# Row 0 of the outer points by four column products, with sums and doublings moved to accumulating DMAs

## The chip, the core and the metric

The kernel runs on one core of one Trainium2 chip. A core has a matmul engine (TensorE, PE), VectorE (DVE), ScalarE (ACT), GpSimd (POOL) and SyncE (SP), each with a queue of its own that it works off in order, and sixteen DMA engines. Accumulating DMAs are issued from POOL, plain loads and stores from SP. The metric is the time of one execution on the device in microseconds. The profile shows one further execution.

## The reference, cut to what matters

Two layers over x of shape (16, 128, 64, 64), each behind a group norm (32 groups):

```
x = x + conv(gn(x))        # 128 to 128 channels, 3x3; inputs quantized, v + 0.1 v^3; three weight sets
x = x + attention(gn(x))   # per position: exp(B) mixes exp(k) v and exp(k), times q, 128 x 64 products
# conv: mem = adc(o[2]) + 4 adc(o[0]) + 2 adc(o[1]) + adc(o[2]);  conv = mem * output_factor + bias
```

`o[i]` is the convolution of the same quantized input with weight set i. `adc` rounds and clips to an 8-bit-step value.

## The kernel before

**Tiling.** One image after another; channels lie on the 128 partitions. The 3x3 convolution is a fast convolution in rows: four output rows (r = 0 to 3) come from six *points* (0 to 5), each a combination of input rows. Points 1 to 4 are the inner ones, 0 and 5 the outer ones. Along a row, columns go in pairs, even and odd.

*Inner points* use four *column products* each. VectorE makes from a point the sums `cs`, the differences `cq` and the shifted differences `cd` of even and odd columns (L509 to L520), and PE forms four matmuls of 128x512 with weights `us` (q1, q2, q0, q3; `Block.half`, L569). *Outer points* use five matmuls: one on `sv`, the sum of even and odd columns (`pairs`, L522; `shared`, L620), whose result `spread` adds to both columns together with sums of the inner points (L623), and four on `v` (`outer`, L627).

For each image there are three *blocks*, one for each weight set. In the block's first part, PE makes points 2 and 1 (h = 0) and 4 and 3 (h = 1) in the PSUM tiles `pa` and `pb`; ACT copies partial sums (m1, sd, sA), and DVE combines them into `ss` (Bo, sm) and `ds` (df). The sum sm for h = 0 is an accumulating DMA on POOL (L596), that for h = 1 a DVE addition (L594). In the second part (`rest`, L645), rows 1 and 2 come from `middle` (ma, mc, L606), and rows 0 and 3 from the PSUM tile `py`:

| name | row 0 (k even) | row 3 (k odd) | engine |
|---|---|---|---|
| S0 / S3 | `total`: adds ss[0][:, 1] to ss[1][:, 1] | `total`: d0 + 8 d1 | DVE (L615, L618) |
| P | shared matmul | the same | PE |
| bc | spread: py + ss[1][:, 1] | py + d0 | DVE (L625) |
| o0, o1 | four matmuls | the same | PE |
| tk | take: py to int16 rows, every second element | the same | ACT (L633) |

The index k is 2i + h. The rest of block i of an image runs as k = 2, 3 (i = 0), 4, 5 (i = 1) and, in the turn of the next image, 0, 1 (i = 2). bA and bB clip the int16 rows (`bound`, L636). aA and aB (`add`, L640) double them on VectorE for block 0, which writes straight to `acc`, and add them to `acc` by an accumulating DMA for the others.

**Around it.** When `acc` is complete, ACT turns it into x (cx, L699), POOL adds the input by DMA (cd0x to cd3x, L702), ACT squares it (sq), DVE and PE make the norm (y0, ya to yd), and four pairs of tiles go through the attention (xn, kp, vp, ek, ekv, dn, g, u, ln, ex, oa, ob, oc, qp, op, r, rd, st; `Pair`, L734). `py` serves these pairs too (qp and op). At the same time the next image is loaded (li, lj), normalized (xa to xd), quantized (n), clipped (cl), made into values (s, va) and combined into rows (gr, er), points (pa, pb, p0, p5) and columns (cs, cq, cd, e0, e5).

**Order.** The order of all these operations is written out: `ORDER` (L38) is the steady turn of one image, `FIRST` and `LAST` the first and last images. A name with "+1" belongs to the turn before. Each engine gets its instructions in that order, so an instruction that waits holds all that stand behind it on its engine. In `Last` (L665) the last block of the last image uses `py` for row 0 and `pb` for row 3.

Of the kernel before, what the change touches and what calls it, by code (L numbers as in the profile page):

```python
# [38 lines left out]
    S3.2+1 cl1+1 q31.2+1 q10.3+1 cl0+1 P.2+1 sA1.2+1 q11.3+1 m10.3+1 bc.2+1 q20.3+1 o1.2+1 s1+1  # L39
    m11.3+1 s0+1 Bo.2+1 sd0.3+1 sq1+1 va1+1 lj3+1 q21.3+1 o0.2+1 va0+1 sd1.3+1 q30.3+1 sq2+1  # L40
    q00.3+1 q01.3+1 tk.2+1 lj2+1 sq3+1 df.2+1 er0+1 sA1.3+1 gr0+1 sA0.3+1 n3+1 P.3+1 ya+1 q31.3+1
    bc.3+1 pmy+1 yb+1 n2+1 q11.4+1 st2+1 sm.2+1 q10.4+1 pvy+1 m10.4+1 o1.3+1 o0.3+1 Bo.3+1 yc+1
    m11.4+1 df.3+1 yl+1 cp+1 yd+1 xn0+1 tk.3+1 ma.4+1 sm.3+1 q20.4+1 cl3+1 kp0+1 vp0+1 ek0+1
    q21.4+1 mc.4+1 st3+1 cl2+1 sd0.4+1 bA.2+1 s3+1 S0.4+1 P.4+1 li0 xn1+1 s2+1 sd1.4+1 ekv0+1
    bc.4+1 va3+1 q00.4+1 va2+1 dn0+1 g0+1 o0.4+1 o1.4+1 li1 q01.4+1 u0+1 ln0+1 oa0+1 tk.4+1 q30.4+1
    S3.4+1 kp1+1 gr1+1 qp0+1 vp1+1 ex0+1 sA0.4+1 sx0 sA1.4+1 ob0+1 q31.4+1 bA.4+1 sx1 oc0+1 ek1+1
    op0+1 er1+1 aA.2+1 q11.5+1 r0+1 q10.5+1 Bo.4+1 ekv1+1 m11.5+1 P.5+1 pa0+1 q21.5+1 x0 bc.5+1
    pb0+1 m10.5+1 dn1+1 q20.5+1 rd0+1 g1+1 sy1 o1.5+1 o0.5+1 st0+1 sd0.5+1 u1+1 oa1+1 cs0+1 df.4+1
    ln1+1 sd1.5+1 q00.5+1 ex1+1 tk.5+1 ob1+1 q30.5+1 cd0+1 qp1+1 q01.5+1 q31.5+1 sy0 xn2 oc1+1
    cq0+1 sA1.5+1 Bo.5+1 op1+1 kp2 sA0.5+1 bB.3+1 vp2 aA.4+1 q10.0 q11.0 df.5+1 r1+1 li3 bB.5+1 ek2  # L50
    m10.0 P.0 aB.3+1 sm.5+1 ekv2 sm.4+1 m11.0 q20.0 q21.0 rd1+1 dn2 mc.0 S0.0 sd0.0 sd1.0 q00.0
    bc.0 li2 g2 q30.0 sx3 aB.5+1 u2 oa2 pb1+1 o1.0 o0.0 ln2 pa1+1 sA0.0 ex2 sx2 q31.0 tk.0 q01.0
    ob2 st1+1 xn3 ma.0 qp2 kp3 oc2 op2 cs1+1 sy3 r2 vp3 S3.0 ek3 bA.0 sA1.0 q10.1 sy2 P.1 Bo.0
    q11.1 ekv3 m10.1 bc.1 dn3 cq1+1 aA.0 g3 o0.1 u3 o1.1 cd1+1 ln3 oa3 lj1 q20.1 ex3 m11.1 tk.1 ob3
    rd2 q21.1 qp3 lj0 bB.1 sd0.1 sd1.1 xa aB.1 q00.1 oc3 op3 q01.1 sA0.1 p0 r3 q10.2 sA1.1 e0 pmx
    df.0 p5 q30.1 rd3 q31.1 m10.2 cx0 e5 xb pvx sm.0 cx1 q11.2 y0 Bo.1 q20.2 cx2 xc m11.2 xl q21.2
    sd0.2 cd0x df.1 q00.2 cx3 sm.1 xd sd1.2 cd2x mc.2 q01.2 cd1x ma.2 S0.2 n1 cd3x sA0.2 n0 sq0
    q30.2
# [4 lines left out]
    hs0+2 x0+2 hq0+2 hs1+2 hq1+2 hq2+2 hq3+2 W0a+2 W0A+2 hs2+2 hs3+2 xa+2 W1a+2 pmx+2 xb+2  # L63
    pvx+2 W2a+2 xc+2 xl+2 hi+2 xd+2 W0b+2 W0c+2 hn1+2 hn0+2 W0e+2 W2A+2 hc0+2 hc1+2 W0d+2 W0f+2
    hn3+2 W2f+2 li0+1 hc3+2 hr1+2 hv1+2 hr0+2 hv0+2 li1+1 W2c+2 W0j+2 er0+2 hn2+2 W0g+2 W1A+2
    sx0+1 sx1+1 W0i+2 gr0+2 W0J+2 cp+2 W0k+2 hc2+2 hr3+2 W1c+2 W0h+2 W1b+2 x0+1 hr2+2 hv3+2
    W1e+2 W1J+2 hv2+2 W0n+2 W0l+2 hb+2 er1+2 sy1+1 W1f+2 gr1+2 W1j+2 li3+1 W0m+2 W0p+2 W0o+2
    pb1+2 hz1+2 hz0+2 sy0+1 li2+1 sx2+1 sy2+1 hcs1+2 hcs0+2 q11.0+1 hcq1+2 hcq0+2 pa1+2 sx3+1
    q10.0+1 sy3+1 m11.0+1 xa+1 W1d+2 W2b+2 hcd0+2 q21.0+1 cs1+2 m10.0+1 W1g+2 q20.0+1 sd0.0+1
    sd1.0+1 W2d+2 hcd1+2 lj0+1 W1h+2 q01.0+1 q30.0+1 q00.0+1 W2e+2 W2g+2 W1i+2 sA1.0+1 cd1+2  # L70
    sA0.0+1 pmx+1 W2h+2 q31.0+1 q11.1+1 m11.1+1 xb+1 cq1+2 q10.1+1 W1l+2 m10.1+1 q21.1+1 lj1+1
    Bo.0+1 W2J+2 pvx+1 W2j+2 q20.1+1 sd0.1+1 q00.1+1 sd1.1+1 q01.1+1 W1k+2 q30.1+1 df.0+1 xc+1
    W1m+2 q31.1+1 p0+1 xl+1 W1o+2 W1n+2 xd+1 sA0.1+1 e0+1 n1+1 P.2+1 sm.0+1 q10.2+1 W1p+2 W2i+2
    Bo.1+1 W2l+2 n0+1 sA1.1+1 df.1+1 q11.2+1 m10.2+1 q20.2+1 sd0.2+1 cl0+1 q00.2+1 sm.1+1
    m11.2+1 ma.2+1 q21.2+1 sA0.2+1 sd1.2+1 q10.3+1 mc.2+1 q01.2+1 p5+1 s0+1 cl1+1 S0.2+1
    q30.2+1 q31.2+1 va0+1 s1+1 S3.2+1 sA1.2+1 lj3+1 W2m+2 q11.3+1 W2n+2 m10.3+1 Bo.2+1 bc.2+1
    m11.3+1 q20.3+1 bA.2+1 va1+1 df.2+1 q21.3+1 lj2+1 e5+1 sd0.3+1 sd1.3+1 n3+1 o1.2+1 n2+1
    o0.2+1 q00.3+1 gr0+1 q30.3+1 q31.3+1 sA0.3+1 q01.3+1 tk.2+1 P.3+1 W2p+2 li0+0 er0+1 sA1.3+1
    W2o+2 q10.4+1 Bo.3+1 sm.2+1 cp+1 bc.3+1 df.3+1 q11.4+1 m11.4+1 o0.3+1 cl2+1 cl3+1 W2k+2
    sx0+0 sm.3+1 s2+1 va2+1 mc.4+1 ma.4+1 q21.4+1 m10.4+1 q20.4+1 sd0.4+1 o1.3+1 sd1.4+1 S0.4+1  # L80
    aA.2+1 x0+0 q30.4+1 li1+0 tk.3+1 S3.4+1 q00.4+1 sA0.4+1 q31.4+1 P.4+1 bc.4+1 s3+1 q01.4+1
    q10.5+1 Bo.4+1 o1.4+1 bB.3+1 va3+1 sx1+0 bA.4+1 er1+1 m10.5+1 q20.5+1 sA1.4+1 aA.4+1 sy1+0
    q11.5+1 m11.5+1 o0.4+1 gr1+1 sd0.5+1 li3+0 tk.4+1 sy0+0 q21.5+1 P.5+1 q00.5+1 sd1.5+1
    q01.5+1 df.4+1 pb0+1 sA1.5+1 q30.5+1 sA0.5+1 q31.5+1 bc.5+1 pa0+1 o1.5+1 Bo.5+1 cq0+1
    df.5+1 cs0+1 o0.5+1 li2+0 tk.5+1 P.0+0 q10.0+0 sm.4+1 m10.0+0 q11.0+0 m11.0+0 sm.5+1
    q20.0+0 sd0.0+0 q21.0+0 sd1.0+0 cd0+1 q01.0+0 mc.0+0 aB.3+1 S0.0+0 bB.5+1 bc.0+0 sx2+0
    pa1+1 ma.0+0 pb1+1 q00.0+0 sA0.0+0 q30.0+0 o0.0+0 S3.0+0 o1.0+0 sy2+0 q31.0+0 aB.5+1 cs1+1
    sx3+0 sy3+0 bA.0+0 aA.0+0 tk.0+0 P.1+0 sA1.0+0 q11.1+0 q10.1+0 m10.1+0 lj1+0 bc.1+0 o0.1+0
    Bo.0+0 m11.1+0 cq1+1 lj0+0 xa+0 o1.1+0 tk.1+0 cd1+1 bB.1+0 aB.1+0 q20.1+0 sd0.1+0 pmx+0
    xb+0 ho+2 q21.1+0 p5+0 sd1.1+0 q00.1+0 pvx+0 xc+0 q01.1+0 p0+0 sA0.1+0 df.0+0 q10.2+0  # L90
    sA1.1+0 q11.2+0 q30.1+0 xl+0 q31.1+0 m10.2+0 q20.2+0 m11.2+0 e5+0 e0+0 cx0+0 Bo.1+0 y0+0
    cx1+0 sm.0+0 cx2+0 sd0.2+0 df.1+0 cd0x+0 cx3+0 q21.2+0 cd1x+0 cd2x+0 q00.2+0 xd+0 sd1.2+0
    sm.1+0 mc.2+0 q01.2+0 sA0.2+0 n1+0 n0+0 q30.2+0 ma.2+0 sq0+0 cd3x+0 S0.2+0
# [4 lines left out]
    cl0+2 sA1.2+2 S3.2+2 q31.2+2 lj3+2 st2+2 q10.3+2 cl1+2 P.2+2 bc.2+2 m10.3+2 q11.3+2 m11.3+2  # L98
    s0+2 q20.3+2 q21.3+2 o0.2+2 Bo.2+2 va0+2 s1+2 va1+2 sd0.3+2 o1.2+2 bA.2+2 sd1.3+2 q01.3+2
    sq1+2 sq2+2 lj2+2 gr0+2 sq3+2 q30.3+2 q00.3+2 tk.2+2 sA1.3+2 er0+2 q31.3+2 sA0.3+2 ya+2  # L100
    df.2+2 n3+2 n2+2 pmy+2 yb+2 P.3+2 bc.3+2 Bo.3+2 cp+2 q11.4+2 pvy+2 q10.4+2 yc+2 cl3+2
    df.3+2 o0.3+2 m10.4+2 m11.4+2 o1.3+2 q20.4+2 q21.4+2 yl+2 s3+2 yd+2 xn0+2 sd0.4+2 sd1.4+2
    kp0+2 vp0+2 sm.3+2 tk.3+2 P.4+2 q01.4+2 cl2+2 sm.2+2 ek0+2 va3+2 mc.4+2 s2+2 st3+2 aA.2+2
    S0.4+2 ekv0+2 bc.4+2 dn0+2 sA1.4+2 g0+2 q00.4+2 sA0.4+2 va2+2 u0+2 xn1+2 ln0+2 o1.4+2 gr1+2
    o0.4+2 q30.4+2 oa0+2 ex0+2 kp1+2 er1+2 tk.4+2 qp0+2 ob0+2 vp1+2 q11.5+2 ma.4+2 oc0+2 S3.4+2
    ek1+2 m11.5+2 pb0+2 op0+2 r0+2 ekv1+2 q31.4+2 Bo.4+2 rd0+2 q10.5+2 pa0+2 m10.5+2 st0+2
    P.5+2 q20.5+2 df.4+2 bc.5+2 sd0.5+2 q21.5+2 sd1.5+2 dn1+2 q00.5+2 g1+2 bB.3+2 xn2+1 bA.4+2
    q01.5+2 q30.5+2 o1.5+2 o0.5+2 u1+2 cs0+2 oa1+2 ln1+2 cd0+2 q31.5+2 ex1+2 tk.5+2 sA1.5+2
    sA0.5+2 cq0+2 aB.3+2 sm.4+2 kp2+1 qp1+2 vp2+1 ob1+2 ek2+1 aA.4+2 Bo.5+2 oc1+2 q10.0+1 op1+2
# [34 lines left out]
def conv_preact_kernel(  # L144
# [29 lines left out]
    P = 128  # L174
# [21 lines left out]

    v = buf("v", 2, T, RW)
    cd = buf("cd", 4, T, 2 * W2)  # L200
    cs = buf("cs", 4, T * W2)
    cq = buf("cq", 4, T * W2)
# [755 lines left out]
```

## Time and profile before

| | us |
|---|---|
| runs | 1602.0, 1598.37, 1602.01 (median 1602.0) |
| the profiled execution, its own time | 1598.49 |
| its span, first to last instruction | 1596.8 |
| PE busy in the span | 1487.7 |
| VectorE busy | 1479.8 |
| ScalarE busy | 1183.0 |
| GpSimd busy | 224.0 |

The granted TensorE clock is 0.981 over the span, and 1.00 in the stretch from 349.1 to 1305.4 us. DMA moved 227 MB, 42.1% of the sixteen engines' span on the queue that POOL writes (software) and 17.9% on SP's (hardware).

How to read it: busy time is the union of an engine's instructions; neighbours overlap a little, so the step from one start to the next is shorter than a duration. One float32 matmul of the program is two records on PE. Waits are put down to what ended last. A DMA's landing time runs from its issue to its end.

### The profile page before, as it was taken

The numbers are of one execution on the slowest core, as the hardware profiler recorded it, in microseconds if no ns is written. First come the engines' busy times: TensorE is split into PE (matmuls) and PEld (weight loads), VectorE is DVE, ScalarE is ACT, GpSimd is POOL, SyncE is SP. The second block draws the span as 40 slices with busy tenths as digits, with TensorE's granted clock in tenths as the row PEclk, the third lists the DMA queues.
The fourth block names the chain that finished last, engine by engine and source line by source line (L and its number), as shares of the span: only waits on it lengthen the run. The fifth ranks groups of instructions, "written<-read, shape, count | busy, mean of one in ns | idle before, by whom it ended". The sixth has DMA issues, their size and how long they took to land.

```text
span 1596.8 us, 14936 instructions
## 1 busy us (share of the span) xinstructions
PE 1487.7 (93%) x4680; PEld 563.4 (35%) x4680; DVE 1479.8 (93%) x1919; ACT 1183.0 (74%) x1857; POOL 224.0 (14%) x250
## 2 busy tenths in 40 slices
PE   1798999999999999999999999999999999999985
PEld 0233433333333333333333343333333333333321
DVE  7999999999999999999999999999999999998775
ACT  7656878787777878778787877878778787766655
POOL 2001011121201112020111201111120111202010
PEclk6899999999999999999999999999999999999998
DMA  6235467594746758465684746659474675836462
GB/s 186 79 92 120 103 160 171 126 204 114 148 128 164 184 119 196 120 137 141 150 205 109 156 131 150 166 132 203 117 152 132 156 176 121 196 66 119 119 158 80
DMA packets 67361, 227.03 MB, mean 142 GB/s; under 512 B 7632, under 2 KB 8272, under 8 KB 67280
## 3 DMA queue, kind: packets, MB, share of 16 engines
q0 software_dynamic: 37904, 123.42, 42.1%
q1 hardware_dynamic: 29088, 101.59, 17.9%
q10 hardware_dynamic: 288, 1.05, 0.2%
q8 instruction: 37, 0.61, 0.2%
q14 instruction: 44, 0.36, 0.1%
HBM read 102.30 MB, written 33.55 MB: 85 GB/s over the span
## 4 chain that ended last, share of the span: by engine, by line
PE 58%; DMA 14%; issue 11%; DVE 11%; ACT 5%; POOL 2%; DVEq 0%; POOLq 0%; ACTq 0%; SPq 0%
PE py L556 19%; PE pa L556 18%; DMA x<-in_x_dram 5%; PE pz L749 5%; PE pb L556 5%; PE pz L759 3%; PE py L749 3%; DMA s<-s 3%; DMA acc<-y 3%; PE py L771 3%; ACT x L699 2%; DVE acc L610 1%; ACT gs L364 1%; DVE y L610 1%; DVE s L615 1%
## 5 line engine op out<-in xcount | busy, mean ns | idle before, releaser
L556 PE MATMUL py<-v,ud 128*128 128x512 f32 x760 | 357.0, 608 | 1.9 <-DVE py L625 1.3
L556 PE MATMUL pa<-cs,us 128*128 128x512 f32 x384 | 199.1, 620 | 41.7 <-DVE cs L514 31.9
L556 PE MATMUL pa<-cd,us 128*128 128x512 f32 x384 | 203.9, 622 | 11.7 <-ACT pb L581 11.7
L556 PE MATMUL pa<-cq,us 128*128 128x512 f32 x384 | 198.1, 612 | 11.3 <-ACT d L579 11.2
L556 PEld LDWEIGHTS py<-v,ud 128*128 128x128 f32 x760 | 138.9, 189 | 184.0 <-issue 148.9
L556 PE MATMUL pb<-cd,us 128*128 128x512 f32 x384 | 194.5, 602 | 1.9 <-ACT pb L581 1.7
L579 ACT ACTIVATE d<-pa 128x512 f32<-128x512 f32 x192 | 112.2, 594 | 37.8 <-PE pa L556 28.0
L812 POOL DMA_DIRECT2D xn<-x x60 | 59.9, 998 | 567.8 <-ACT xn L782 567.5
L581 ACT ACTIVATE pb<-pa 128x512 f32<-128x512 f32 x192 | 112.5, 586 | 31.3 <-PE pa L556 30.7
L584 ACT ACTIVATE s<-pa 128x512 f32<-128x512 f32 x192 | 110.4, 591 | 32.0 <-PE pa L556 29.9
L749 PE MATMUL pz<-xn,w 128*64 128x512 f32 x480 | 121.8, 607 | 1.3 <-ACT xn L796 1.2
L587 DVE SCALAR_TENSOR_TENSOR s<-d,pb 128x1024 f32<-128x1024 f32 x96 | 117.2, 1221 | 3.6 <-PE pb L556 3.2
L643 POOL DMA_DIRECT2D acc<-y x62 | 68.5, 1105 | 360.8 <-DVE y L636 212.2
L588 DVE TENSOR_TENSOR d<-s 128x1024 f32<-128x1024 f32 x96 | 117.5, 1224 | 1.6 <-ACT s L584 1.5
L633 ACT ACTIVATE y<-py 128x1024 int16<-128x1024 f32 x63 | 84.0, 1334 | 46.0 <-PE py L556 44.8
L782 ACT ACTIVATE xn<-py,scalars 128x512 f32<-128x512 f32 x120 | 76.0, 685 | 56.1 <-PE py L771 56.0
L556 PEld LDWEIGHTS pa<-cs,us 128*128 128x128 f32 x384 | 66.3, 191 | 139.6 <-issue 67.0
L556 PEld LDWEIGHTS pa<-cq,us 128*128 128x128 f32 x384 | 68.0, 190 | 119.5 <-issue 69.4
L556 PEld LDWEIGHTS pa<-cd,us 128*128 128x128 f32 x384 | 66.4, 190 | 123.6 <-ACT pb L581 56.9
L556 PEld LDWEIGHTS pb<-cd,us 128*128 128x128 f32 x384 | 70.2, 190 | 96.0 <-issue 85.2
L556 PE MATMUL py<-sv,ud 128*128 128x512 f32 x190 | 97.7, 596 | 3.3 <-ACT y L633 3.2
L596 POOL DMA_DIRECT2D s<-s x48 | 45.9, 956 | 339.5 <-DVE d L588 127.9
(224 smaller groups left out, 2651.8 us busy)
## 6 DMA issues: line engine op xcount, KB each, us to landing
xc<-in_x_dram SPq DMA_DIRECT2D x121, 512.0 KB, 5.6
acc<-y POOLq DMA_DIRECT2D x62, 512.0 KB, 5.5
x<-in_x_dram POOLq DMA_DIRECT2D x60, 512.0 KB, 10.4
xn<-x POOLq DMA_DIRECT2D x60, 512.0 KB, 4.9
out_dram<-xn SPq DMA_DIRECT2D x60, 512.0 KB, 5.1
s<-s POOLq DMA_DIRECT2D x48, 512.0 KB, 6.3
gmat<-in_x_dram SPq DMA_DIRECT2D x5, 512.0 KB, 8.9
x<-in_g_neg_dram SPq DMA_DIRECT2D x2, 576.0 KB, 11.4
```

The lines of the kernel that those rows point to most:

```text
L556: pe.matmul(o if len(r.shape) == 2 else o.rearrange("p (t w) -> p t w", w=W2), w, r, start=start, stop=stop, skip_group_check=True,)
L579: f"m1{u}.{k}": lambda u=u, a=a: act.activation(d[:, u], a, AF.Copy),
L581: f"sd{u}.{k}": lambda a=a, b=b: act.activation(b, a, AF.Copy, scale=-1.0),
L584: f"sA{u}.{k}": lambda u=u, a=a: act.activation(s[:, u, 0], a, AF.Copy),
L587: f"Bo.{k}": lambda: dve.scalar_tensor_tensor(s[:, :, 1], d, 2.0, pb, ALU.mult, ALU.add),
L588: f"df.{k}": lambda: dve.tensor_tensor(d, s[:, 1], s[:, 0], ALU.subtract),
L633: act.activation(self.column(self.part(1)[0], h), y, AF.Copy)
L643: pool.dma_start(a, y, accum_op=ALU.add)
L749: pe.matmul(self.tiles(o)[h * IC : (h + 1) * IC], w, x[:, t[0] : t[1] : t[2]], start=True, stop=True)
L759: pe.matmul(o[c, t], eb[r, c], self.half(x)[r, t], start=True, stop=True, skip_group_check=True)
L782: act.activation(g[:, t], self.tiles(self.op[h]), AF.Identity, bias=bias_sb)
L812: "rd": lambda: pool.dma_start(self.r, self.x2, accum_op=ALU.add),
```

## The change

Row 0 of each block now takes the point 0 like an inner point. VectorE makes for it a fifth set of `cs`, `cq` and `cd` (e0, w0, c0) in place of its part of `sv`; the weights `us` get a fifth row, and `ud` keeps only the outer point 5. In `py`: P is the product with `cs`; C (VectorE) adds twice that to the second column of z = ss[1][:, 1]; o2 adds the product with `cq` to the first half of `py`; se (ACT) copies that, negated, into the second half; o0 and o1 add the products with `cd`; tk (VectorE) adds z and writes the int16 row. bc and ACT's take are gone for row 0. S0 becomes an accumulating DMA on POOL (after mc and C, before tk), except in the last block. The doubling of block 0's rows is an accumulating DMA of `acc` onto itself. In the last block, row 3 has its shared matmul twice, into both halves of `pz`, and VectorE adds and writes in one step. `ORDER`, `FIRST` and `LAST` are written anew.

```diff
-    v = buf("v", 2, T, RW)
-    cd = buf("cd", 4, T, 2 * W2)
-    cs = buf("cs", 4, T * W2)
-    cq = buf("cq", 4, T * W2)
-    sv = buf("sv", 2, T * W2)
+    v = buf("v", T, RW)
+    cd = buf("cd", 5, T, 2 * W2)
+    cs = buf("cs", 5, T * W2)
+    cq = buf("cq", 5, T * W2)
+    sv = buf("sv", T * W2)
...
-    us = [buf(f"us_{i}", 4, 4, C) for i in range(3)]
+    us = [buf(f"us_{i}", 5, 4, C) for i in range(3)]
...
-                "j": lambda: outer(0),
-                "J": lambda: outer(1),
+                "j": lambda: copy(u[:, 4, 0:3], g0, AF.Copy, scale=0.25),
+                "J": outer,
...
-        def total(self, h):
-            if h == 0:
+        def total(self, h, vector=False):
+            if h == 0 and (vector):
                 dve.tensor_tensor(ss[1][:, 1], ss[0][:, 1], ss[1][:, 1], ALU.add)
+            elif h == 0:
+                pool.dma_start(ss[1][:, 1], ss[0][:, 1], accum_op=ALU.add)
             else:
...
+        def zero(self):
+            w, z = us[self.i][:, 4], ss[1][:, 1]
+            return {
+                "P": lambda: mm(py[:, 0], w[:, 1], cs[:, 4], True, True),
+                "C": lambda: dve.scalar_tensor_tensor(z[:, 1], py[:, 0], 2.0, z[:, 1], ALU.mult, ALU.add),
+                "o2": lambda: mm(py[:, 0], w[:, 2], cq[:, 4], False, True),
+                "se": lambda: act.activation(py[:, 1], py[:, 0], AF.Copy, scale=-1.0),
+                "o0": lambda: mm(py[:, 0], w[:, 0], cd[:, 4, :, W2 : 2 * W2], False, True),
+                "o1": lambda: mm(py[:, 1], w[:, 3], cd[:, 4, :, 0:W2], False, True),
+                "tk": lambda: dve.tensor_tensor(self.column(self.part(1)[0], 0), py, z, ALU.add),
+            }
...
         def add(self, y, a):
-            if self.i == 0:
-                dve.tensor_scalar(y, y, 2.0, None, ALU.mult)
-            else:
-                pool.dma_start(a, y, accum_op=ALU.add)
+            pool.dma_start(a, y, accum_op=ALU.add)
...
+                "tP1": lambda: [self.shared(pz, c) for c in range(2)],
+                "tp0": lambda: self.outer(0, pz), "tp1": lambda: self.outer(1, pz),
+                "tk3": lambda: dve.tensor_tensor(self.column(self.part(1)[0], 1), pz, self.d[0], ALU.add),
...
-            o["p0"] = lambda: inputs[c].point(0, v[:, 0])
-            o["e0"] = lambda: inputs[c].pairs(0)
+            z = f[:, 0:T]
+            o["p0"] = lambda: inputs[c].point(0, z)
+            for e, g in inputs[c].columns(slice(4, 5), z).items():
+                o[{"cs": "e0", "cq": "w0", "cd": "c0"}[e]] = g
```

The new `ORDER` around row 0, for k = 4, 0 and 2:

```
mc.4+1 cl2+1 vp0+1 s3+1 sd0.4+1 C.4+1 li0 q00.4+1 va3+1 ek0+1 s2+1 sd1.4+1 ekv0+1 bB.3+1 va2+1 o2.4+1 dn0+1 S0.4+1 sA0.4+1 se.4+1
g0+1 q30.4+1 q01.4+1 S3.4+1 sx1 oa0+1 o1.4+1 u0+1 q10.5+1 aA.2+1 xn1+1 ln0+1 o0.4+1 kp1+1 gr1+1 tk.4+1
...
C.0 g2 pb1+1 sd1.0 pa1+1 sx3 u2 q00.0 o2.0 q30.0 ma.0 rd1+1 se.0 o1.0 o0.0 oa2 q01.0 cs1+1 sA0.0 S0.0 ln2 q31.0 q10.1 ex2 tk.0
...
cd0x n0 q00.2 mc.2 cd1x sA0.2 C.2 ma.2 q21.2 y0 S0.2 n1 cl0 q10.3 cl1 bA.2 o2.2 sd1.2 se.2 q30.2 o1.2 S3.2 cd2x s1 s0 m10.3 o0.2 q01.2 sq0 q20.3 sA1.2 q31.2 va1 q11.3 sq1 va0 cd3x tk.2
```

## The prediction

> **What bounds the kernel now.** First the page's busy line and its slices.
>
> ```profile
> PE 1487.7 (93%) x4680; PEld 563.4 (35%) x4680; DVE 1479.8 (93%) x1919; ACT 1183.0 (74%) x1857; POOL 224.0 (14%) x250
> PE   1798999999999999999999999999999999999985
> DVE  7999999999999999999999999999999999998775
> ```
>
> TensorE (PE) and VectorE (DVE) are both full from about 120 us to 1500 us, ScalarE (ACT) is not. So the price lies in the steady part. Its period is 95.6 us per image: POOL's s<-s transfer sm.2 (L596) is issued at 826.20 us in one image and at 921.83 in the next. Next, ten periods as one stage:
>
> ```profile
> 349.10:1305.40 956.30, 933.77 (x2951) 354.38 (x2950) 913.63 (x1181) 745.15 (x1169) 140.14 (x151) 1.00 0.65 152
> ```
>
> The columns are PE, weight loads, DVE, ACT, POOL, granted clock, DMA share, GB/s. Per image PE is busy 93.4 us, DVE 91.4, ACT 74.5; the DMA engines are 65% busy. Then what DVE and PE waited for in that stage:
>
> ```profile
> DVE ekv L809 <- PE py L749: 13.5, 10, 1.4
> DVE acc L610 <- DMA s<-s: 9.1, 8, 1.4
> DVE y L368 <- ACT gs L364: 4.4, 4, 1.7
> DVE y L360 <- ACT x L699: 4.1, 5, 1.6
> PE pa L556 <- ACT d L579: 8.1, 10, 2.1
> PE pa L556 <- ACT s L584: 5.0, 7, 1.0
> ```
>
> All DVE waits come to 31.8 us in ten periods, 3.2 per image, so DVE is occupied 92.4 of 95.6 us: 91.4 of busy time and 1.0 of small gaps. PE's waits are 2.2 per image. Neither waits long; the two pass work to each other and both are near their limit.
>
> What an instruction takes from a full engine is the step to the next start, not its duration:
>
> ```profile
> 876.75 1.23 DVE L625 TENSOR_TENSOR py<-py,s 128x1024 f32<-128x1024 f32 x1
> 877.89 0.68 DVE L804 TENSOR_TENSOR ek<-gs,pz 128x512 f32<-128x512 f32 x1
> 878.49 0.68 DVE L807 TENSOR_TENSOR ekv<-gs,pz 128x512 f32<-128x512 f32 x1
> ...
> 878.26 3.67 PE L556 MATMUL py<-v,ud 128*128 128x512 f32 x8
> 881.77 1.02 PE L556 MATMUL pb<-cd,us 128*128 128x512 f32 x2
> 882.62 1.02 PE L556 MATMUL pa<-cd,us 128*128 128x512 f32 x2
> ```
>
> DVE: 1.14 us for 128x1024, 0.60 for 128x512. PE (two records are one matmul of the program): 3.51 us for the four outer matmuls, 0.86 for a column product.
>
> The Trainium skill, "Perfetto Trace Analysis", section "Identifying the Most-Contended Engine", calls matmul busy time a poor measure, and occupancy a fair one for VectorE. It speaks against pricing this change by PE: by DVE alone, step 2 below with all waits kept, the gain would be 0.9 us per image.
>
> **The change part by part**, per image of three blocks; all five parts lie in the full stage.
>
> 1. *PE.* Per block the shared matmul and four outer ones (0.86 + 3.51 = 4.37) become four column products (4 x 0.86 = 3.44): 0.93 less, 2.8 per image. The emitted order shows one more hand-over per block: o2 waits for DVE's C, as o0 waits for ACT's se, where before only the first of four waited for DVE. A group that follows a hand-over took up to 3.78 where it else took 3.51, so 0 to 0.27 each; I take 0.2. PE: -2.2 us (bounds -2.8 and -2.0).
>
> 2. *DVE.* Removed: three spreads bc (1.14 each, L625), three sums S0 (L615, 128x1024, 1.13) and two doublings (L641, 0.60 each): 8.0. Added: w0 (0.60, as sv in L525), c0 (128x1024 elements, 1.13), three C, three additions tk. C reads 128x512 from PSUM: 0.60 as L804. tk reads PSUM, as L625 (1.14), and writes every second int16, as L610 (1.26 step, 1.37 long): between, 1.20. Sum 0.60 + 1.13 + 1.80 + 3.60 = 7.1. Net -0.9; with tk at 1.14 to 1.37 and C up to 0.75 (L787) the bounds are -1.1 and +0.1. DVE occupied: 92.4 - 0.9 = 91.5.
>
> 3. *ACT.* Three takes of 1.33 go, three copies se of 0.59 come: -2.2. ACT has 21 us free per image, so nothing; its saving also covers se, which stands between o2 and o0.
>
> 4. *POOL and DMA.* Five more accumulating transfers of 512 KB: three S0, two doublings. POOL: 15 issues per image become 20, about 1 us each, on an engine 14% busy: nothing by itself, but its queue is in order. DMA: the software queue took 45.9% of 1100 us for 177 issues, 2.85 us of all sixteen engines each. Five more make 14 us, 65% becomes 80%. Landing before:
>
> ```profile
> xc<-in_x_dram SPq DMA_DIRECT2D x92, 512.0 KB, 6.0
> x<-in_x_dram POOLq DMA_DIRECT2D x48, 512.0 KB, 10.4
> acc<-y POOLq DMA_DIRECT2D x47, 512.0 KB, 5.8
> s<-s POOLq DMA_DIRECT2D x35, 512.0 KB, 6.6
> ```
>
> The doublings stand in POOL's queue close ahead of the next accumulation into the same rows. aA of k=2 is issued behind S0 of k=4; aA of k=4 must wait for bA anyway, 10.8 us of DVE work after C. aB of k=3 has about 8 us of DVE work (pb0, df, oa1, u1, cs0, cd0, cq0) until bB of k=5. Against 5.8 to land (longest 8.8) both are hidden. Late by 1 or 2 us, aB of k=5 would hold rd1 and S0 of k=0 behind it, which have 6.5 us: still nothing. If all that cover were gone, a doubling would cost what it lands late, up to 9 us.
>
> 5. *The new wait.* tk adds z = ss[1][:,1], which S0 changes by DMA. S0 cannot be issued before C has written z, and tk waits for its landing. DVE is in order, so behind tk everything on DVE stands: S3, bound, Bo, and so pa, pb and d for PE. The cover is the DVE work written between C and tk, by the steps above:
> - rest k=4: va3, ekv0, bB, va2, S3, oa0, u0, gr1 = 8.4 us
> - rest k=0: pb1, pa1, u2, ma, oa2, cs1 = 6.0 us
> - rest k=2: ma, y0, cl0, cl1, bA, S3, va1, va0 = 6.4 us
>
> s<-s landed in 4.5 to 7.9, median 6.6, plus 0.1 for the semaphore. k=4 is covered. k=0 lacks 0 to 2.0, by the median 0.7. For k=2, POOL has issued cd0x and cd1x some 5 us earlier (loads of x added from DRAM, 8.2 to 11.8 to land when four come together), so S0 can queue behind them: it lacks 0 to 5.5. By the s<-s row it would be 0.3, by the cd row up to 5.4; nearest is s<-s issued close behind other transfers of its queue (7.7), so 1.3, less what DVE waits for anyway in between. Together I take 1.6 per image, bounds 0 and 7.5.
>
> Here the Trainium skill has a price: "DMA: Bandwidth & Descriptors", "Anatomy of one DMA", fits 2.0 us plus bytes over 436 GB/s, an estimate of 3.2 us for 512 KB. By it all three covers hold and the term is 0; the rows of s<-s, never under 4.5, decide against it.
>
> POOL's queue moves too: cd2x and cd3x now stand behind S0 of k=2, which waits for C. Their squares feed ya on DVE 13 us of work after C; cd3x issued 2 us after C and landing in 8 to 12, with the square's 1.3, needs 11.5 to 15.5. L368 waits 0.4 per image for this now; I keep 0.4 and put the excess into the range.
>
> Other waits: the one of L809 for PE (1.35) shrinks to about 0.5, since PE loses more work than DVE; the one of mc for sm (0.9) goes, as sm.0 has 13 us of DVE work behind it; the two of the norm stay (0.85).
>
> *Ends.* The start is bound by DVE. Three weight sums for each of three weights work on five rows instead of four (a step of 0.60 becomes some 0.75), the differences on half as much, and w0 and c0 come before anything is saved: about +1.5 us. At the end, spread (1.25), four matmuls (3.79) and take (1.31) become C, o2, se, o0, o1 and tk: 0.6 + 0.9 + 0.6 + 1.7 + 1.2 and 0.2 for each of five hand-overs, much the same; the other row loses its spread (1.22): about -1.5. Together 0, bounds -3 and +3.
>
> **Sum.** DVE 91.5 + waits 0.5 + 0.85 + 1.6 = 94.4 us, against 95.6; PE needs 93.4 - 2.2 + its waits 2.2 = 93.4, less, so DVE sets it. 1.2 us x 15 periods = 18 us. The profiled execution spans 1596.8 and took 1598.5 as a run; the runs' median is 1602.0. 1598.5 - 18 = 1580.5; I say 1581.
>
> **Rivals.**
> - *PE's relief decides.* S0 lands in time everywhere and waits fall to those of the norm: DVE 91.5 + 0.85 + 0.5 = 92.8, PE 91.2 + 1.6. 2.8 x 15 = 42 us: 1557. For it: L809's wait is PE's lateness. Against it: covers of 6.0 and 6.4 against 6.6. Chance 0.16.
> - *Nothing is won.* The transfers, 80% instead of 65% busy, each land a little later, and the wait of tk and those of the accumulated row (acc, x, norm) take 2.4 to 3 us instead of 1.6. Time 1594 to 1603. Chance 0.13.
> - *S0's landing holds DVE (slower).* One mechanism: S0 of k=2 behind cd0x and cd1x. From 2.8 us of waiting at tk per image (91.5 + 1.35 + 2.8 = 95.6) the gain is gone. At a landing of 9.8, between 7.8 and 11.8, it lacks 3.5, with k=0's 1.3 it is 4.8: 2.0 x 15 = 30 us, 1629. For it: 80% DMA share and the neighbours on the queue. Against it: the cds start 5 us earlier, and at 2.85 us of service each the two are nearly through. Chance 0.20.
> - That the change does not do what it says is excluded by the emitted order: 25 matmuls per block instead of 26, three takes on DVE.
>
> **Numbers.** The forecast (1568 to 1592) has 0.51, the rest as above. About 0.3% (5 us) is what a measurement can tell from no change. Faster 0.67, same 0.13, slower 0.20. The range goes from 1557 to 1625; left out are the worst half of the slower case and little below.
>
> **What would show it.** Right: a period near 94.4; DVE busy near 90.5 and PE near 91 per image; L809's wait halved; a line of tk (L647) waiting for DMA s<-s, 1 to 2 us per image, at k=0 and k=2. Wrong: no such line and a period under 93.5 (PE's relief), or over 3 us of it per image (slower); tk longer than 1.4; s<-s landing later than 8.

## The result and the profile after

The changed kernel takes 1657.6 us (median of 4 runs, 1653.7 to 1662.0); the kernel before, on the same chip, 1602.0. The ratio is 1.035 (95% interval 1.032 to 1.038). The forecast was 1581 with a range to 1625: the direction was wrong, and the time lies outside the range.

The profiled execution after spans 1654.3 us at a mean granted clock of 0.965 (before: 1596.8 at 0.981). I take the period from the start of the first load cd0x of one image to that of the next, as the mean of all 14 intervals. Before it is 94.44 us, after 97.57: 3.1 us per image, 44 us in all. Another 5.4 us come before the first of these loads (149.11 us before, 154.49 after); the rest of the 57.5 us of span, 8, comes behind the last, where DVE waits 6.4 us for S0 of k=2 of the last turn.

The changed kernel's busy line and its slices, to be read against those of before:

```profile
PE 1475.8 (89%) x4586; PEld 550.3 (33%) x4586; DVE 1467.9 (89%) x1920; ACT 1146.1 (69%) x1850; POOL 301.5 (18%) x329
PE   1788999989999898998989899898998989898985
DVE  7998998989989898998989899898998989898675
```

Work went away, as planned: PE and DVE are each 12 us less busy over the run. But the unbroken rows of nines are broken by eights, in both engines alike. Each image now has a place where both stand still. The stretch of before, in the same columns (PE, weight loads, DVE, ACT, POOL, granted clock, DMA share, GB/s):

```profile
349.10:1305.40 956.30, 887.91 (x2784) 331.93 (x2784) 870.24 (x1126) 694.63 (x1119) 181.29 (x193) 0.98 0.77 172
```

These are 9.80 periods, 10.13 before. DVE is busy 88.8 us per image (before 90.2), PE 90.6 (92.2), and the DMA engines 77% (65%). What DVE waited for in that stretch (us in all, times, longest):

```profile
DVE y L368 <- ACT gs L364: 31.3, 10, 4.8
DVE acc L647 <- DMA s<-s: 22.0, 10, 3.4
DVE ekv L824 <- PE py L764: 8.6, 15, 0.7
DVE s L642 <- PE py L556: 2.7, 8, 0.5
DVE y L647 <- DMA s<-s: 2.4, 5, 1.0
```

Line numbers have moved: L824 is the ekv of L809, L642 is C, L647 is tk. `acc` in L647 is k=2, `y` are k=4 and k=0. The waits for PE fell (13.5 to 8.6). New are tk's, 2.2 us per image at k=2 and only 0.2 at the two other places, and the wait of L368, the sum of squares for the norm, which grew from 0.4 to 3.2 us. All of DVE's waits, the smaller ones that are not shown included, make 75.5 us in the stretch, 7.7 per image, where they made 31.8, or 3.1: +4.6, less the 1.4 us of busy time saved, is the +3.1 of the period within 0.1.

One image shows how the two waits hang together. POOL's timeline (start, us, engine, line, operation, tiles, count, and in brackets the idle time before it with what ended it), then DVE's and ACT's:

```profile
835.44 1.76 POOL L717 DMA_DIRECT2D x<-in_x_dram  x2 [2.81 <-ACT x L714]
840.94 0.85 POOL L616 DMA_DIRECT2D s<-s  x1 [3.73 <-DVE s L642]
841.48 2.33 POOL L717 DMA_DIRECT2D x<-in_x_dram  x2
```

```profile
839.95 0.69 DVE L642 SCALAR_TENSOR_TENSOR s<-py,s 128x512 f32<-128x512 f32 x1
...
849.62 1.30 DVE L647 TENSOR_TENSOR acc<-py,s 128x1024 int16<-128x1024 f32 x1 [2.69 <-DMA s<-s]
...
859.05 0.16 DVE L368 TENSOR_REDUCE y<-y 128x2 f32<-128x8 f32 x1 [2.77 <-ACT gs L364]
```

```profile
849.61 0.60 ACT L584 ACTIVATE s<-pa 128x512 f32<-128x512 f32 x1 [2.93 <-DMA s<-s]
...
857.78 1.15 ACT L364 ACTIVATE gs<-x,y 128x1024 int16<-128x1024 f32 x1 [1.16 <-DMA x<-in_x_dram]
```

POOL has issued cd0x and cd1x and then stands 3.73 us in front of S0, which waits for DVE's C. cd2x and cd3x stand behind it. Their data (ACT's L714) was ready from 838.15 us on; they are issued at 841.48. S0 lands 8.6 us after its issue, and two engines wait for that: DVE at tk, and ACT at L584, whose copy overwrites the source that S0 is still reading. The later load is the last to land:

```profile
842.01 15.68 DMA x<-in_x_dram
```

This line is from the chain of waits: 15.7 us where I had taken 8 to 12. In the kernel before, the four loads of one image went out like this, and the last line gives the landing of the fourth alone (count, KB, us):

```profile
904.15 0.85 POOL L702 DMA_DIRECT2D x<-in_x_dram  x1 [0.78 <-ACT x L699]
906.41 1.73 POOL L702 DMA_DIRECT2D x<-in_x_dram  x2 [1.42 <-ACT x L699]
908.86 0.85 POOL L702 DMA_DIRECT2D x<-in_x_dram  x1 [0.72 <-ACT x L699]
...
x<-in_x_dram POOLq DMA_DIRECT2D x1, 512.0 KB, 14.2
```

So the fourth load landed late before the change too: at 923.1, its square ended at 924.3, and L368 started at 924.39. Its reader had nothing to spare. Over the 15 images it was issued 4.7 us behind the first load and landed in 14.0 (medians; landing 12.6 to 15.2); after the change it is 6.6 and 15.5. So 1.9 us of delay come from the place behind S0 and 1.5 from the slower landing.

After the change ACT squares the load (1.25 us), and only then DVE can form the norm. From C at 839.95 to L368 at 859.05 are 19.1 us. DVE has 13.6 us of work in them; 2.69 and 2.77 are waits. So in this image the loads alone set these 5.4 us: with the same landing and no wait at tk, L368 would have waited that much longer.

### The profile page after: what moved, and what is told of

It is laid out like the page before. It is cut to its first block, busy times and chain, and to the rows that moved or that the text cites. A ratio compares the mean times of both kernels' runs of the same rounds, so it can differ in the third digit from the quotient of the medians.

```text
span 1654.3 us, 14852 instructions
## 1 busy us (share of the span) xinstructions
PE 1475.8 (89%) x4586; PEld 550.3 (33%) x4586; DVE 1467.9 (89%) x1920; ACT 1146.1 (69%) x1850; POOL 301.5 (18%) x329
## 4 chain that ended last, share of the span: by engine, by line
PE 33%; DMA 25%; DVE 17%; issue 7%; ACT 5%; POOL 2%; SPq 0%; DVEq 0%; POOLq 0%; ACTq 0%
DMA x<-in_x_dram 11%; PE pa L556 10%; PE py L556 8%; DMA acc<-y 4%; PE pb L556 4%; PE pz L764 3%; DMA xc<-in_x_dram 3%; DMA xn<-x 3%; DMA s<-s 3%; PE pz L774 2%; PE py L786 2%; PE py L764 2%; POOL x L717 2%; DVE d L588 2%; DVE y L610 1%
## 5 line engine op out<-in xcount | busy, mean ns | idle before, releaser
L556 PE MATMUL pa<-cs,us 128*128 128x512 f32 x384 | 213.2, 641 | 72.1 <-ACT s L584 40.5
L556 PE MATMUL pa<-cq,us 128*128 128x512 f32 x384 | 210.5, 634 | 13.5 <-ACT d L579 13.5
L556 PE MATMUL pa<-cd,us 128*128 128x512 f32 x384 | 202.5, 611 | 7.0 <-ACT pb L581 7.0
L556 PE MATMUL pb<-cd,us 128*128 128x512 f32 x384 | 204.4, 617 | 0.0
L556 PE MATMUL py<-v,ud 128*128 128x512 f32 x376 | 182.4, 615 | 0.6 <-DVE py L626 0.6
L584 ACT ACTIVATE s<-pa 128x512 f32<-128x512 f32 x192 | 112.9, 589 | 90.7 <-PE pa L556 53.9
L656 POOL DMA_DIRECT2D acc<-y x62 | 63.8, 1030 | 389.3 <-DVE y L651 222.6
L556 PEld LDWEIGHTS pa<-cs,us 128*128 128x128 f32 x384 | 67.1, 194 | 183.3 <-issue 72.2
L588 DVE TENSOR_TENSOR d<-s 128x1024 f32<-128x1024 f32 x96 | 116.9, 1218 | 5.3 <-ACT s L584 5.0
L556 PEld LDWEIGHTS pa<-cd,us 128*128 128x128 f32 x384 | 70.1, 194 | 117.9 <-issue 63.1
L556 PEld LDWEIGHTS pa<-cq,us 128*128 128x128 f32 x384 | 68.2, 196 | 113.9 <-ACT d L579 50.7
L596 POOL DMA_DIRECT2D s<-s x48 | 41.7, 870 | 352.4 <-DVE d L588 312.9
L556 PEld LDWEIGHTS pb<-cd,us 128*128 128x128 f32 x384 | 66.8, 191 | 97.3 <-issue 70.9
L556 PE MATMUL py<-cd,us 128*128 128x512 f32 x192 | 95.5, 606 | 3.3 <-ACT py L644 3.3
L556 PEld LDWEIGHTS py<-v,ud 128*128 128x128 f32 x376 | 69.9, 193 | 85.2 <-issue 72.0
L616 POOL DMA_DIRECT2D s<-s x47 | 40.8, 869 | 284.3 <-DVE s L642 269.4
L516 DVE TENSOR_TENSOR cd<-f 128x2048 f32<-128x2048 f32 (+1 forms) x47 | 90.2, 1920 | 0.0
```

Source lines behind the costliest of these rows:

```text
L516: "cd": lambda: dve.tensor_tensor(cd[:, k].rearrange("p i t w -> p (i t) w"), z[:, :, 0 : 2 * W2], z[:, :, 1 : 2 * W2 + 1], ALU.subtract,),
L556: pe.matmul(o if len(r.shape) == 2 else o.rearrange("p (t w) -> p t w", w=W2), w, r, start=start, stop=stop, skip_group_check=True,)
L584: f"sA{u}.{k}": lambda u=u, a=a: act.activation(s[:, u, 0], a, AF.Copy),
L588: f"df.{k}": lambda: dve.tensor_tensor(d, s[:, 1], s[:, 0], ALU.subtract),
L596: pool.dma_start(s[:, 1], s[:, 0], accum_op=ALU.add)
L616: pool.dma_start(ss[1][:, 1], ss[0][:, 1], accum_op=ALU.add)
```

## Experiments

**Theory A**: the place of S0 of k=2 is the price, by POOL's order (loads behind it, it behind C) and by its landing. **Rival B**: the load is the price; five more transfers per image keep all landings late, whatever stands where. A third question was what the four products themselves are worth. All diffs are against the changed kernel unless said otherwise. Times are medians; ratios are to the kernel before, run beside them (1598.4 to 1599.3 us), with 95% intervals. The waits are those of the stretch 349.1 to 1305.4.

### S0 of k=2 on VectorE

```diff
-            if h == 0 and (vector):
+            if h == 0 and (vector or self.i == 0):
```

> The changed kernel, but S0 of k=2 (block 0) is a VectorE addition again; S0 of k=4 and k=0 and the doublings stay DMAs. In the changed kernel a period is 97.65 us, and per image VectorE waits 3.1 us for the squares (L368), 2.1 us at tk for S0, and ACT 2.4 us for S0 before it may write its source ss[0] (L584), which PE sees as 2.7 us. Theory A (S0 of k=2 and the two loads cd2x, cd3x behind it in POOL's queue cost the time): L368's wait falls to about 0.4, the others go, VectorE gains 1.13 of work: period 97.65 - 2.7 - 2.1 + 1.1 = 94.0, time about 1600. Theory B (all transfers land later because the DMA engines are 77% busy instead of 65%): one transfer of eight new ones is gone per image... of five new ones, so a fifth of 55 us comes back: 1646. Theory C (the chain P, C, o2, se, o0, o1, tk over three engines costs it): no gain, 1655 to 1670.

Measured: **1594.6 us**, ratio 0.9967 (0.9951 to 0.9983), period 93.32. One of five new transfers undone, and 63 us come back; this is 0.3% faster than before. Stage and DVE waits:

```profile
349.10:1305.40 956.30, 916.91 (x2919) 342.25 (x2918) 925.56 (x1206) 732.45 (x1181) 178.53 (x192) 1.00 0.78 176
```

```profile
DVE ekv L824 <- PE py L764: 9.2, 15, 0.7
DVE d L588 <- ACT s L584: 2.9, 2, 1.5
...
DVE y L647 <- DMA s<-s: 1.6, 5, 0.5
```

The DMA engines are as busy as after the change (78%, 77%) and move more per second. So the mean load is not the price, and the longer chain of row 0 over three engines (theory C above) is not either. L368 no longer appears; S0 of k=4 and k=0, still transfers, cost tk 0.16 us per image. The loads go out without the stop:

```profile
900.10 2.61 POOL L717 DMA_DIRECT2D x<-in_x_dram  x3 [2.73 <-ACT x L714]
903.20 0.85 POOL L717 DMA_DIRECT2D x<-in_x_dram  x1 [0.49 <-ACT x L714]
```

### The order of the five transfers turned both ways

cd2x and cd3x ahead of S0:

```diff
-    ... mc.2 cd1x sA0.2 C.2 ma.2 q21.2 y0 S0.2 n1 ... S3.2 cd2x s1 ... va0 cd3x tk.2
+    ... mc.2 cd1x cd2x cd3x sA0.2 C.2 ma.2 q21.2 y0 S0.2 n1 ... S3.2 s1 ... va0 tk.2
```

> The changed kernel with cd2x and cd3x issued ahead of S0 of k=2 in POOL's queue (steady turn only), no other edit. Theory A1 (what costs is that the loads stand behind S0, which waits for C): L368's wait falls from 3.1 to about 0.4 and the time to 1657 - 2.7 x 13 = 1622. Theory A2 (what costs is S0's own landing, which holds tk and the writer of ss[0]): S0 now lands behind four loads, at 11 or more instead of 8.6 to 9.1, so tk and ACT wait 2 to 3 us more and PE with them: 1657 to 1690. Theory B (load): no change within 5 us.

cd0x and cd1x behind S0:

```diff
-    ... cd0x n0 q00.2 mc.2 cd1x sA0.2 C.2 ma.2 q21.2 y0 S0.2 n1 ...
+    ... n0 q00.2 mc.2 sA0.2 C.2 ma.2 q21.2 y0 S0.2 cd0x cd1x n1 ...
```

> The changed kernel with cd0x and cd1x issued behind S0 of k=2 (steady turn only), so that all four loads stand behind it. S0 should land in 5 to 6 us: tk's wait (2.1) and ACT's (2.4) go, while the loads start about 5 us later than now. Theory A1 (the loads' start): L368 waits longer, 3.1 becomes 6 or more, time 1660 to 1690. Theory A2 (S0's landing): the gain of 2.1 to 2.7 per image outweighs it, 1625 to 1645. Theory B (load): no change within 5 us.

Measured: 1724.7 us (1.079, 1.076 to 1.082) and 1716.3 us (1.073, 1.071 to 1.076), both far worse than the change and outside every range given, those of theory A included. With the loads first, S0 lands late:

```profile
DVE acc L647 <- DMA s<-s: 87.6, 10, 9.9
DVE y L368 <- ACT gs L364: 17.0, 9, 2.4
```

With S0 first, the loads do, ACT stands in front of them in its order, and PE and DVE behind ACT:

```profile
ACT gs L364 <- DMA x<-in_x_dram: 101.6, 25, 8.2
```

```profile
DVE py L626 <- PE py L556: 63.6, 10, 7.4
DVE y L368 <- ACT gs L364: 23.1, 9, 2.7
```

So neither turn helps: each makes one part of the five transfers wait out the others, and both parts have a reader on a full engine. Other orders were not run. By the prediction's own 2.85 us of all sixteen engines for each, five take 14.3 us where DVE has 13.6 us of work behind C; this is rough, since cd0x and cd1x start 4.5 us ahead of C and other queues move data beside them.

### Half of S0 of k=2

The first of its two columns on VectorE, the second by a transfer of 256 KB:

```diff
+            elif h == 0 and self.i == 0:
+                dve.tensor_tensor(ss[1][:, 1, 0], ss[0][:, 1, 0], ss[1][:, 1, 0], ALU.add)
+                pool.dma_start(ss[1][:, 1, 1], ss[0][:, 1, 1], accum_op=ALU.add)
```

> The changed kernel, but of S0 of k=2 the first column (ss[0][:, 1, 0], which ACT overwrites in the next half) is added by VectorE (0.6 us) and only the second column by DMA (256 KB). ACT no longer waits for the DMA before it writes ss[0]; tk still waits for it, and cd2x and cd3x still stand behind it. Theory A3 (the held source, seen by ACT and then PE, is what costs): 2.7 us per image come back less 0.6, about 1625. Theory A4 (tk's wait and the loads behind it are what cost): the smaller transfer lands perhaps 1 us earlier, 1640 to 1655.

Measured: 1653.0 us (1.033, 1.029 to 1.036), as the change. What went and what stayed:

```profile
DVE y L368 <- ACT gs L364: 32.4, 10, 4.3
...
DVE acc L650 <- DMA s<-s: 3.0, 6, 0.9
```

tk's wait is down from 22.0 to 3.0, and ACT's for the held source no longer appears, but the time hardly moves (by about 4 us, inside the intervals). The fourth load lands 1.1 us earlier (median 14.4 against 15.5) and DVE has its 0.6 us of addition to do in between; the rest of what tk no longer waits L368 waits instead, so its row stays where it was. PE's wait for the held source (`PE pa L556 <- ACT s L584`) falls from 27.2 to 5.9 us, and its wait for the norm (`PE pz L383 <- DVE y L378`) grows from 20.0 to 30.2. So the landing at tk and the held source do not set the time by themselves; what is left is the loads behind the sum.

### S0 of k=2 computed by GpSimd, ahead of and behind the loads

```diff
+            elif h == 0 and self.i == 0:
+                pool.tensor_tensor(ss[1][:, 1], ss[0][:, 1], ss[1][:, 1], ALU.add)
```

> The changed kernel with S0 of k=2 computed by GpSimd itself instead of by a transfer. If the landing of S0 and the loads behind it are the price, and GpSimd adds 128x1024 float32 in under 3 us: 1580 to 1600, below the run with this sum on VectorE (1594.6), because VectorE loses 1.13 us per image. If GpSimd takes 5 us or more, or slows VectorE beside it, cd2x and cd3x stand behind it as behind the transfer, the wait of L368 comes back, and it is 1610 to 1660.

The second run has the same sum, and the order of the first run above (cd2x and cd3x ahead of S0):

> As the run with S0 of k=2 computed by GpSimd (1648.8 us), but with the loads cd2x and cd3x ahead of it in POOL's queue; the operations are the same, only that place changes. If the place of the two loads behind a sum that waits for C is the price of the change, the wait of L368 (4.8 us) goes and, with VectorE still held some 2 us per image while GpSimd adds, the time is 1590 to 1615. If the loads were late for the traffic of the DMA engines, which stays the same, it is 1640 to 1655.

Measured: 1648.8 us (1.030, 1.026 to 1.034) ahead of the loads, **1609.8** (1.006, 1.005 to 1.008) behind them. Here S0 of k=2 is no transfer, tk of k=2 waits for nothing in either run, the operations are the same, and 39 us hang on the place of two loads in POOL's queue. Ahead of them, DVE's largest wait is again

```profile
DVE y L368 <- ACT gs L364: 25.2, 10, 4.8
```

and behind them that line is gone. This shows the price of that place when GpSimd computes the sum. In the changed kernel itself S0 is also a fifth transfer, and no run divides the 63 us between its place and its traffic. The 15 us that remain against the sum on VectorE are DVE held by GpSimd; see the last section.

### The doublings back on VectorE

```diff
-            pool.dma_start(a, y, accum_op=ALU.add)
+            if self.i == 0:
+                dve.tensor_scalar(y, y, 2.0, None, ALU.mult)
+            else:
+                pool.dma_start(a, y, accum_op=ALU.add)
```

> The changed kernel with the doublings back on VectorE (two passes of 0.60 us per image), everything else as changed. Theory A: they have nothing to do with the loss; VectorE has 7.5 us of waits per image, so its 1.2 us of work are partly absorbed: 1650 to 1675. Theory B (DMA load, 77% becomes about 71%): two of the five new transfers go, so some 20 us come back: 1635 or less.

Measured: 1673.2 us (1.045, 1.042 to 1.048), 15.6 us worse than the change, with three transfers more than before instead of five. Rival B falls a second time: the doublings as transfers are a gain, near the 2 x 0.60 us x 14 = 17 us that they take off DVE.

### How many S0 should be transfers

All three on VectorE (`if h == 0:`), then those of k=2 and k=0 (`self.i != 1`):

> The changed kernel with all three S0 as VectorE additions; the doublings stay DMAs. With S0 of k=2 alone on VectorE the time was 1594.6 and VectorE was 96.8% busy. Theory A (only S0 of k=2 hurt, the DMAs of k=4 and k=0 are covered and save VectorE work): two more passes of 1.13 on a full VectorE, +2.3 us per image, about 1628. Theory B (any S0 as a DMA costs something): faster than 1594, down to 1585.

> The changed kernel with S0 of k=2 and of k=0 on VectorE and only that of k=4 by transfer. If VectorE sets the pace once k=2 is repaired, each sum on it costs 1.13 us by 14 to 15 periods, 17 us: 1604 to 1612, half way between 1594.6 (only k=2 on VectorE) and 1618.5 (all three). If k=0's cover of 6.0 us was too short as forecast (0.7 us per image), the wait saved there is taken off: 1596 to 1602.

Measured: 1618.5 us (1.012, 1.010 to 1.014) with all three on VectorE, 1600.9 (1.000, 0.999 to 1.002) with only k=4 as a transfer, against 1594.6 with k=4 and k=0. The transfer of k=4 is worth 17.6 us, a whole VectorE addition per image (1.13 x 15 = 17). (With all three on VectorE I had said 1628, 10 us too much.) That of k=0 is worth 6 us, a third of it. In the stretch DVE's waits come to 19.3 us with that transfer and to 13.7 without, 0.5 us per image, which is most of what is missing; but only 0.16 us of it names S0, and why the others grow stays open.

### The products alone

All S0 and both doublings on VectorE:

> The changed kernel with S0 and the doublings all on VectorE: what is left is the row 0 by four column products, tk on VectorE and the new order. VectorE has 0.60 + 1.13 + 3 x (0.60 + 1.20) - 3 x 1.14 = +3.7 us more per image than the kernel before, PE 2.2 less. Theory D (VectorE is the bound): slower than the kernel before by 2.5 to 3.7 us per image, 1635 to 1655. Theory P (PE is the bound): faster than the kernel before, 1570 to 1595.

Measured: 1634.9 us (1.022, 1.020 to 1.025). In the stage DVE is as full as it gets, and PE has room:

```profile
349.10:1305.40 956.30, 891.34 (x2845) 332.77 (x2843) 930.58 (x1201) 710.72 (x1145) 133.44 (x148) 1.00 0.64 148
```

Per image PE is busy 2.5 us less than in the kernel before (89.7 against 92.2) and DVE 3.4 more (93.6 against 90.2; by step 2's prices 3.7). With the new order, the products lose 2.2%. So what the change can win comes from the sums that leave DVE. The products make room on PE, and the next pair of runs shows what two of those sums are worth without that room.

### The doublings as transfers in the kernel before

Diff against the kernel before:

```diff
-            if self.i == 0:
-                dve.tensor_scalar(y, y, 2.0, None, ALU.mult)
-            else:
-                pool.dma_start(a, y, accum_op=ALU.add)
+            pool.dma_start(a, y, accum_op=ALU.add)
```

> The kernel before with the doublings alone as accumulating DMAs; nothing else is edited, its order stays. VectorE has 1.2 us less per image, the DMA engines two more transfers (65% to about 71%). Theory D (VectorE sets the pace of the kernel before): 10 to 18 us faster, 1580 to 1588. Theory P (PE does): no change, 1594 to 1600. Theory B (load): slower, 1605 or more.

Measured: 1679.8 us (1.050, 1.048 to 1.053). I had not expected a loss of 81 us from two transfers. POOL's timeline of this run gives the reason:

```profile
915.05 1.55 POOL L640 DMA_DIRECT2D acc<-acc  x1 [12.13 <-DVE acc L636]
915.76 1.76 POOL L596 DMA_DIRECT2D s<-s  x1
```

The doubling aB.3 waits 12 us for its clip bB.3 (L636), and the sum sm.4 (L596), whose data DVE's L588 had written from 906.81 to 908.03, stands behind it and is issued at 915.76. DVE then waits 5 us for that sum. The mending run moves aB.3 behind sm.4; of the names that it passes, only sm.4 is POOL's:

```diff
-    m10.0 P.0 aB.3+1 sm.5+1 ekv2 sm.4+1 m11.0 q20.0 q21.0 rd1+1 ...
+    m10.0 P.0 sm.5+1 ekv2 sm.4+1 aB.3+1 m11.0 q20.0 q21.0 rd1+1 ...
```

> The kernel before with its two doublings by accumulating DMA, as in the run that took 1680 us, but aB.3 moved two names in the order, behind sm.4, so that POOL no longer waits for bB.3 ahead of issuing the sum sm.4 (issued 8.9 us after its data was ready there). If the place in POOL's queue is the price: the wait of L610 for s<-s (5.4 us, 8 times in ten periods) goes, 80 us come back, and with two DVE instructions of 0.60 less per image the time is 1585 to 1605. If the transfers' load on the DMA engines is the price, it stays at 1660 to 1685, since the same transfers run.

Measured: 1600.8 us (1.001, 0.999 to 1.003): 79 us hang on the order of two issues in POOL's queue. And although DVE is busy 1.2 us less per image, nothing is won against before: its waits grow by the same 1.2 us (31.8 to 43.8 in the stretch), and PE is 97% busy in the stage. That fits PE setting the time there.

```profile
349.10:1305.40 956.30, 932.22 (x2948) 353.37 (x2947) 901.75 (x1160) 744.33 (x1167) 161.73 (x171) 1.00 0.71 162
```

Less work for DVE alone gains nothing, less for PE at DVE's cost loses 2.2%, both together (S0 of k=2 on VectorE) gain 0.3%. That is the best version run.

## Why the prediction was wrong

- **The frame held, its base did not.** "DVE sets it", occupied time plus waits: right for the changed kernel; in the kernel before, 1.2 us less on DVE won nothing. But the period of 95.6 us was one long image; the mean of 14 is 94.44, so the 94.4 that I forecast for the changed kernel is what the kernel before had. The waits per image stood (3.1), so DVE is occupied 91.3, not 92.4.
- **Step 1, PE -2.2.** PE's busy time fell by 39.6 us over 16 images where nothing stalls (1448.1, S0 of k=2 on VectorE), 2.5 per image. Right. Its rival, "PE's relief decides" (42 us), is not borne out: in that run PE is relieved, DVE is as busy per image as before (90.3 against 90.2) and waits little for S0, and the period falls by 1.1 us, not by 2.8.
- **Step 2, DVE -0.9.** The span has 11.9 us less, 0.7 per image; in the steady stage it is 1.4. tk steps 1.20 (849.62 to 850.82), as taken, C 0.61 against 0.60. Right.
- **Step 3, ACT -2.2.** 36.9 us over 16 images, 2.3. Right.
- **Step 4, doublings hidden.** They land in 6.9 us, later than the 5.8 taken, and no wait names them. DMA share 77% against 80%. Right; in the kernel before, where the order was not made for them, they cost 81 us, and the bound "up to 9 us" did not think of what stands behind a waiting issue.
- **Step 5, tk's wait.** k=4 covered, right. k=0: 0.7 taken, at most 0.2 measured. k=2: 1.3 taken, 2.2 measured, S0 landing in 6.2 to 9.3, median 8.5, where I took 7.7. That ACT would have to wait for the tile that S0 reads was not in the prediction.
- **The step that failed: "POOL's queue moves too".** I wrote that cd3x, "issued 2 us after C and landing in 8 to 12, with the square's 1.3, needs 11.5 to 15.5" of 13 us of cover, kept 0.4 and "put the excess into the range". Issue (2.1), square (1.25) and cover (13.6) are as written; the landing was 15.7, so the need is 19.0, and L368 waits 3.2 per image. With it goes the wait at tk, inside the same 5.4 us.

  The number was in the profile of the kernel before. "8.2 to 11.8" is not what four loads together took there, 6.6 to 15.2; the row's median of 10.4 mixes all four, and the one that counts, the fourth, took 14.0. With 14.0 the need is 2 + 14.0 + 1.3 = 17.3, or 4.3 more than the 13 us of cover, and 0.4 could not be kept. The other 1.5 us go with S0's own transfer: with S0 of k=2 on VectorE the fourth load landed in 14.1. Full DMA engines are no sign of it by themselves. Before the change their share (second last column) was as high while the fourth load moved, and PE and DVE were busy (first row); after it, both mostly stand (second row):

```profile
915.00:925.00 10.00, 9.97 (x23) 3.99 (x22) 9.80 (x14) 9.44 (x15) 0.85 (x1) 1.00 1.05 305
...
846.00:850.20 4.20, 1.71 (x4) 0.40 (x3) 1.51 (x2) 1.27 (x4) 0.00 (x0) 1.00 1.05 298
```

- **The slower rival** named the right transfer, S0 of k=2 "behind cd0x and cd1x", and nearly its landing (9.8 against 9). Its price was put at tk, where S0 is read. Half of S0 shows that this wait is not what costs, GpSimd's sum behind the loads shows what does: 1629 was too low because the loads behind S0 were left out of it, and the ends.
- **Ends.** Put at 0, with bounds of 3 either way; 5.4 us came before the first load and 8 behind the last, 13 of the 57.5. Of these, 6.4 are DVE's wait for S0 of the last turn; the start was not taken apart.
- **Put together:** 91.3 - 1.4 + 7.7 of waits = 97.6 against 97.57 measured. On the right base the forecast was 91.3 - 0.9 + 0.5 + 0.85 + 1.6 = 93.4. Against it L368's wait is 2.8 more, tk's 0.9 and the other waits 1.0, and busy time is 0.5 less: the loads behind S0 are most of the error.

## What to carry to other kernels

When a transfer joins an in-order queue, price the instructions behind it as well as its reader: what they wait for now (here C, 3.7 us), and what their own readers have left. Take the landing of the very transfer that is read, here the fourth of four at 14.0 us, not the median of its row at 10.4, and look whether its reader has any time left now, here none. A sum that is cheap to compute (1.13 us) may be worth keeping at the one place where others stand behind it in the queue, and moving at the others.

## What the runs showed of the hardware

*A pause of PE can lower its clock.* After the change PE paused more than 2 us 13 times between 340 and 1440 us; in 10 of these the float32 matmuls that followed took nearly twice as long. One such place (two rows) and one where the clock held (two rows); PE's busy time is the second number, the granted clock the third from the end:

```profile
847.80:851.20 3.40, 0.94 (x2) 0.48 (x3) 1.58 (x2) 1.59 (x3) 0.00 (x0) 1.00 1.05 277
851.20:854.60 3.40, 3.40 (x5) 1.31 (x4) 3.40 (x3) 1.27 (x4) 0.00 (x0) 0.50 1.07 278
943.35:946.77 3.42, 1.79 (x4) 0.48 (x3) 1.27 (x3) 0.89 (x2) 0.00 (x0) 1.00 1.03 271
946.77:950.18 3.41, 1.74 (x4) 0.67 (x4) 2.38 (x3) 2.30 (x4) 0.00 (x0) 1.00 1.06 275
```

```profile
846.69 1.02 PE L556 MATMUL pb<-cd,us 128*128 128x512 f32 x2
850.26 1.21 PE L556 MATMUL pa<-cs,us 128*128 128x512 f32 x2 [2.55 <-ACT s L584]
851.25 1.92 PE L556 MATMUL py<-sv,ud 128*128 128x512 f32 x2
852.96 1.83 PE L556 MATMUL pa<-cq,us 128*128 128x512 f32 x2
```

A pause of 2.55 us, then 1.92 instead of 1.02 for a product of the same shape. After a pause of 3.30 us, at 948.44, it was 1.12 and 1.02. The rows above show the difference. In this trace's clock records the falls lie on a fixed grid of 3.41 us (those at 458.6, 851.2 and 1253.9 us are 115 and 118 steps apart), and what counts is how long PE was busy in one step. A step with 0.94 us was followed by half the clock; the grid cut the pause of 3.30 us into two steps with 1.79 and 1.74, and the clock held. In the traces of all runs, between 200 and 1450 us, every step at full clock with less than 1.35 us of PE busy was followed by half the clock, and none with more than 1.65 us. The Trainium skill, "TensorE: Matmul & The Clock Gate", section "What's actually happening", tells of half the clock after an idle window of some 3.4 us that runs freely; the trace agrees with the window and its length, but the window need not be idle throughout, as the 0.94 us show. A stall thus costs more than its length: the runs with the longest stalls have the lowest clocks (0.941 and 0.944 for the two orders, 0.980 with S0 of k=2 on VectorE). How much of the time this makes was not measured by itself.

*GpSimd holds VectorE.* In the run with S0 of k=2 on GpSimd, an instruction of one element per partition took 2.31 us instead of 0.15, and ended with GpSimd's addition (842.62):

```profile
839.24 3.38 POOL L616 TENSOR_TENSOR s<-s,s 128x1024 f32<-128x1024 f32 x1 [3.57 <-DVE s L644]
840.32 2.31 DVE L360 SCALAR_TENSOR_TENSOR y<-y,x 128x1 f32<-128x1 f32 x1
```

It did so in nearly every image (median 2.32). The Trainium skill, "SBUF — State Buffer", section "SBUF: two separate sides", says that a VectorE instruction with two inputs in SBUF and a GpSimd instruction exclude each other for the whole instruction; the rows agree. It goes both ways. In most images VectorE's L610, with two such inputs, was running when GpSimd's addition began, and the addition took 3.38 us; in the last image the addition began first and took 2.34, and L610 took 3.53 instead of 1.38. The price of that sum is then 2.2 us of DVE, against 1.13 for VectorE to do it: 1.0 x 14 = 15 us, the difference between 1609.8 and 1594.6.

*An accumulating transfer holds its source until it has landed,* by the program's own order: ACT waited 24.9 us in ten images for S0 before it could write into the tile that S0 reads.
